# A later exponential, a sum at the end of the pass, and a shared ring of buffers, in the linear attention layer of a four-layer network

## The chip, the cores and the metric

The kernel runs on one core of a Trainium2 chip. The core has five engines with queues of their own: TensorE (PE, with its weight loads PEld), VectorE (DVE), ScalarE (ACT), GpSimd (POOL) and SyncE (SP, which here only issues transfers). They meet through semaphores. The metric is the device time of one execution in microseconds, the median over several runs.

## The reference

Sixteen images of 4096 tokens with 256 channels pass through four layers. Each is `x = x + layer(groupnorm(x))`:

- layer 0: a search for the nearest of 1024 code vectors for each token
- layer 1: row attention with a sigmoid
- layer 2: a gate from a softmax over all 4096 tokens
- layer 3: linear attention with a layer norm. The change lies in it:

```python
qkv = jnp.einsum('bxyc,cf->bxyf', x, w_qkv)
q, k, v = jnp.split(qkv, 3, axis=-1)
...
q = jax.nn.softmax(q, axis=-2) * SCALE
k = jax.nn.softmax(k, axis=-1)
context = jnp.einsum('bhdn,bhen->bhde', k, v)
out = jnp.einsum('bhde,bhdn->bhen', context, q)
...
out = jnp.einsum('bxyh,hc->bxyc', out, w_out) + b_out
mu = jnp.mean(out, axis=-1, keepdims=True)
var = jnp.mean(jnp.square(out - mu), axis=-1, keepdims=True)
out = (out - mu) * jax.lax.rsqrt(var + LN_EPS) * gamma + beta
```

The softmax of q runs over the 32 channels of a head; that of k over all 4096 tokens.

## The kernel before

All is float32. An image is cut into eight chunks of 512 tokens (`NCHUNK`), a chunk into four tiles of 128 (`CH`). The layers are Python generators (`stage1`, `layer1`, `rows2`, `stage2`, `gate2`, `stage3`), one set for each image. A heap at the end of the kernel steps through the generators of several images by due time: each `yield n` moves its generator on by n units, and a `stage3` has 160 of them (`task("layer3", ..., 160)`). So the search of one image is written between the exponentials of the one before and the attention of an older one. The order in which the code is thus written out is a priority: a planner then lays out each engine's queue, takes ahead what it holds ready, and on the chip each queue runs in the order laid out. Tiles with the same `tag` share `bufs` buffers, which are handed out in the order of the code.

`stage3` has two parts.

The **pass over k** (from L740): for each chunk `xt` is loaded (L742), PE forms k's scores `pk` (L747), DVE takes their maximum into the running `nkm` (L750, L753), ACT forms `al`, the factor by which older sums shrink (L754), and `kx`, the exponential of k, with its sum in `ks` (L756). POOL keeps the running sum: `ksum = ksum * al + ks` (L758, L759). PE forms queries and values, which ACT copies to `qv` (L769 to L774). In the second half of the chunk, after `yield 5`, `kx` is transposed and copied to `ek` (L780, L782). The queries of the chunk before, already normalized, are transposed (`queries`, L726), copied to `qT` (L728) and stored to DRAM by ACT's queue (L730). Then the maximum of this chunk's queries over each head is taken (DVE, L788), subtracted (POOL, L789), and the exponential taken in place (ACT, L790). PE forms `pc`, which joins the context `ctxa` (L794, L796). In the next chunk `normalize` sums the exponentials on DVE (L736), inverts, and multiplies on POOL (L738).

**Between** the parts the context is turned into the output weights `wctx` and their Gram matrix `gram` (L805 to L827), at raised priority; `rk = 1 / ksum` is used at L815.

The **output pass** (from L870): `fetch` loads a chunk of transposed queries back into `qo` (L834, on SP), `form` multiplies it by `gram` on PE (`pz`, L838) and with itself on DVE (`qz`, L840), `variance` sums the squares (L846) and raises to the power -1/2 on POOL (L849), `deviate` scales the queries (L856, L857). For each of two halves (`pr`) PE sums the transposed residual, the product with `wctx` and a row (`pxo`, L884 to L894), ACT copies to `y` (L895), and SP stores it (L905). `form` runs two chunks ahead, `fetch` three.

The tiles `kx`, `ek`, `qT` and `qz` share tag `v2` with four buffers; `qo` has three of its own, each of 2 KB per partition.

Of the kernel before, what the change touches and what calls it, by code (L numbers as in the profile page):

```python
# [9 lines left out]
F32 = mybir.dt.float32  # L10
BF16 = mybir.dt.bfloat16
U32 = mybir.dt.uint32
AF = mybir.ActivationFunctionType
ALU = mybir.AluOpType
AX = mybir.AxisListType

P = 128
# [4 lines left out]
CH = 4  # L22
NCHUNK = NT // CH
CW = CH * P
# [17 lines left out]
def kernel(  # L42
# [7 lines left out]
    nc = tc.nc  # L50
# [10 lines left out]
    s3p = ctx.enter_context(tc.tile_pool(name="s3p", bufs=2))  # L61
# [637 lines left out]
    def stage3(b):  # L699
        tag = f"s3_{b}"  # L700
# [21 lines left out]
        def queries(ch):  # L722
            qv = qvs.pop(ch)
            pq = bank(f"pq_{tag}_{ch}")
            for t in range(CH):
                nc.tensor.transpose(pq[:, t * P : (t + 1) * P], qv[:, t, 0, :], ident)  # L726
            qT = s3p.tile([P, CW], F32, tag="v2", name=f"qT_{tag}_{ch}", bufs=4)
            nc.scalar.activation(qT, pq, AF.Copy, scale=float(DH ** -0.5))  # L728
            qd_ = dram.tile([P, CW], F32, tag=f"qT_{ch}", name=f"qd_{tag}_{ch}")
            nc.scalar.dma_start(out=qd_, in_=qT)  # L730
            qTs.append(qd_)

        def normalize(ch):
            q4 = qvs[ch][:, :, 0, :].rearrange("p t (h d) -> p t h d", d=DH)
            qd = small.tile([P, CH, HEADS], F32, tag="qd", name=f"qd_{tag}_{ch}")
            nc.vector.tensor_reduce(qd, q4, AX.X, ALU.add)  # L736
            nc.vector.reciprocal(qd, qd)  # L737
            nc.gpsimd.tensor_tensor(q4, q4, qd.unsqueeze(3).to_broadcast([P, CH, HEADS, DH]), ALU.mult)  # L738

        for ch in range(NCHUNK):  # L740
            xt = xb.tile([P, NK, CW], F32, tag="xb", name=f"xk_{tag}_{ch}")
            nc.sync.dma_start(out=xt, in_=x3[ch])  # L742
            if ch > 0:
                normalize(ch - 1)
            pk = bank(f"pk_{tag}_{ch}")
            for k in range(NK):
                nc.tensor.matmul(pk, lhsT=wk_n[:, k, :], rhs=xt[:, k, :], start=(k == 0), stop=(k == NK - 1))  # L747

            now = nkm[:, ch : ch + 1]
            nc.vector.tensor_reduce(now, pk, AX.X, ALU.max, negate=True)  # L750
            if ch > 0:
                last = nkm[:, ch - 1 : ch]
                nc.vector.tensor_scalar(now, now, last, None, ALU.min)  # L753
                nc.scalar.activation(al[:, ch : ch + 1], last, AF.Exp, scale=-1.0, bias=now)  # L754
            kx = s3p.tile([P, CW], F32, tag="v2", name=f"kx_{tag}_{ch}", bufs=4)
            nc.scalar.activation(kx, pk, AF.Exp, bias=now, accum_out=ks[:, ch : ch + 1])  # L756
            if ch > 0:
                nc.gpsimd.tensor_tensor(ksum, ksum, al[:, ch : ch + 1], ALU.mult)  # L758
                nc.gpsimd.tensor_tensor(ksum, ksum, ks[:, ch : ch + 1], ALU.add)  # L759
            else:  # L760
                nc.gpsimd.tensor_copy(ksum, ks[:, 0:1])
            qv = s3p.tile([P, CH, 2, P], F32, tag="u4", name=f"qv_{tag}_{ch}")
            qvs[ch] = qv
            for pr in range(CH // 2):
                pqv = bank(f"pqv_{tag}_{ch}_{pr}").rearrange("p (j n) -> p j n", j=2)
                for j in range(2):
                    t = 2 * pr + j
                    for k in range(NK):
                        nc.tensor.matmul(  # L769
                            pqv[:, j, :], lhsT=xt[:, k, t * P : (t + 1) * P], rhs=wqv_n[:, k, :],  # L770
                            start=(j == 0 and k == 0), stop=False, skip_group_check=True,
                        )
                nc.tensor.matmul(pqv, lhsT=ones3, rhs=twice(qv_row), start=False, stop=True, skip_group_check=True)
                nc.scalar.copy(qv[:, 2 * pr : 2 * pr + 2, :, :].rearrange("p j s n -> p j (s n)"), pqv)  # L774
            if ch == 0:
                put_row(x_row, xm_, by_identity, f"x_{tag}", idle=8)
            yield 5
            pkt = bank(f"pkt_{tag}_{ch}")
            for t in range(CH):
                nc.tensor.transpose(pkt[:, t * P : (t + 1) * P], kx[:, t * P : (t + 1) * P], ident)  # L780
            ek = s3p.tile([P, CH, P], F32, tag="v2", name=f"ek_{tag}_{ch}", bufs=4)
            nc.scalar.copy(ek.rearrange("p t d -> p (t d)"), pkt)  # L782
            if ch > 0:
                queries(ch - 1)

            q4 = qv[:, :, 0, :].rearrange("p t (h d) -> p t h d", d=DH)
            qm = small.tile([P, CH, HEADS], F32, tag="qm", name=f"qm_{tag}_{ch}")
            nc.vector.tensor_reduce(qm, q4, AX.X, ALU.max)  # L788
            nc.gpsimd.tensor_tensor(q4, q4, qm.unsqueeze(3).to_broadcast([P, CH, HEADS, DH]), ALU.subtract)  # L789
            nc.scalar.activation(qv[:, :, 0, :], qv[:, :, 0, :], AF.Exp)  # L790

            pc = bank(f"pc_{tag}_{ch}")
            for t in range(CH):
                nc.tensor.matmul(pc[:, :P], lhsT=ek[:, t, :], rhs=qv[:, t, 1, :], start=(t == 0), stop=(t == CH - 1))  # L794
            if ch > 0:
                nc.vector.scalar_tensor_tensor(  # L796
                    ctxa, ctxa, al[:, ch : ch + 1], pc[:, :P], op0=ALU.mult, op1=ALU.add
                )
            else:
                nc.vector.tensor_copy(ctxa, pc[:, :P])  # L800
            yield 5
        normalize(NCHUNK - 1)
        rk = small.tile([P, 1], F32, tag="rk", name=f"rk_{tag}")
        nc.vector.reciprocal(rk, ksum)
        with tc.high_priority(offset=URGENT):  # L805
# [21 lines left out]
            nc.scalar.activation(gram, pw[:, :P], AF.Copy, scale=1.0 / C)  # L827
        yield 4
        queries(NCHUNK - 1)
        qs, prods, rss = {}, {}, {}  # L830

        def fetch(ch):
            qs[ch] = s3p.tile([P, CW], F32, tag="qo", name=f"qo_{tag}_{ch}", bufs=3)
            nc.sync.dma_start(out=qs[ch], in_=qTs[ch])  # L834

        def form(ch):
            pz = bank(f"pz_{tag}_{ch}")
            nc.tensor.matmul(pz, lhsT=gram, rhs=qs[ch], start=True, stop=True)  # L838
            prods[ch] = s3p.tile([P, CW], F32, tag="v2", name=f"qz_{tag}_{ch}", bufs=4)
            nc.vector.tensor_tensor(prods[ch], pz, qs[ch], ALU.mult)  # L840

        def variance(ch):
# [13 lines left out]
                nc.tensor.transpose(pd[:, t * P : (t + 1) * P], rs[:, t : t + 1].to_broadcast([P, P]), ident)  # L856
            nc.vector.tensor_tensor(qs[ch], pd, qs[ch], ALU.mult)  # L857

        fetch(0)
        fetch(1)  # L860
        form(0)
        yield 3
# [9 lines left out]
        for ch in range(NCHUNK):  # L872
            xt = xb.tile([P, NK, CW], F32, tag="xb", name=f"xo_{tag}_{ch}")
            nc.sync.dma_start(out=xt, in_=x3[ch])
            qT = qs[ch]
            y = s3p.tile([P, CH, C], F32, tag="u4", name=f"y_{tag}_{ch}")
            for pr in range(2):
                if pr == 1 and ch + 1 < NCHUNK:
                    deviate(ch + 1)
                px = bank(f"pxo_{tag}_{ch}_{pr}").rearrange("p (j c) -> p j c", c=C)  # L880
                for j in range(2):
                    t = 2 * pr + j
                    for k in range(NK):
                        nc.tensor.matmul(  # L884
                            px[:, j, k * P : (k + 1) * P], lhsT=xt[:, k, t * P : (t + 1) * P], rhs=ident,
                            is_transpose=True, start=(j == 0 and k == 0), stop=False, skip_group_check=True,
                        )
                for j in range(2):
                    t = 2 * pr + j
                    nc.tensor.matmul(  # L890
                        px[:, j, :], lhsT=qT[:, t * P : (t + 1) * P], rhs=wctx[:, 1, :], start=False, stop=False,
                        skip_group_check=True,
                    )
                nc.tensor.matmul(px, lhsT=ones3, rhs=twice(x_row), start=False, stop=True, skip_group_check=True)  # L894
                nc.scalar.copy(y[:, 2 * pr : 2 * pr + 2, :], px)  # L895
                if pr == 0:
                    if ch + 2 < NCHUNK:
                        form(ch + 2)
                else:
                    if ch + 2 < NCHUNK:  # L900
                        variance(ch + 2)
                    if ch + 3 < NCHUNK:
                        fetch(ch + 3)
                    if before is not None:
                        nc.sync.dma_start(out=dst[:, (ch - 1) * CH : ch * CH, :], in_=before)  # L905
                yield 3
            before = y
# [73 lines left out]
```

## Time and profile before

| what | us |
|---|---|
| median of three runs | 5770.42 (5766.87 to 5782.12) |
| the profiled execution | 5760.43 |
| its span in the profile | 5758.7 |
| L756 `kx`, ACT, 128 times, mean | 0.670 |
| L790 exponential of q, ACT, 128 times, mean | 0.627 |
| L789 subtraction, POOL, 128 times, mean | 1.572 |
| L758, L759 sum of k, POOL, 112 times each, mean | 0.906, 0.629 |
| L738 normalization, POOL, 128 times, mean | 1.593 |
| L838 `pz`, PE, all | 147.8 |
| L890 `pxo` with `wctx`, PE, all | 268.5 |
| L630 DVE and L627 ACT of the gate's softmax, 1024 times each, mean | 2.339, 2.089 |

The profile is of one execution. For each engine it gives the busy time, and the idle time before each group of instructions with what ended it. A table of waits sums these by pair ("who waited for whom": total, times, longest). The chain of waits follows the work that ended last back from the last instruction. The timeline lists single instructions, with the idle time before each in brackets. The granted TensorE clock was 0.958 of full speed on average.

### The profile page before, as it was taken

What the parts mean: (1) busy time and instruction counts of PE and PEld (TensorE: products, weight loads), DVE (VectorE), ACT (ScalarE), POOL (GpSimd) and SP (SyncE); (2) the same over time, 40 slices, a digit from 0 to 9 for tenths busy, and PEclk for the clock granted to TensorE, in tenths of its full rate; (3) what the DMA queues carried; (4) which work ended last, traced back from release to release, by engine and by line L of the source; (5) the groups of instructions that cost most, each with busy time, mean ns of one, the idle gap of its engine ahead of it and who ended that gap; (6) DMA issues with size and microseconds to landing.
All of it is one profiled execution on the core that took longest, in us unless ns stands there. A gap on an engine that the chain in (4) does not pass through costs nothing.

```text
span 5758.7 us, 80501 instructions
## 1 busy us (share of the span) xinstructions
PE 5245.1 (91%) x28975; PEld 3212.6 (56%) x28975; DVE 5067.1 (88%) x7154; ACT 4496.9 (78%) x6498; POOL 1930.8 (34%) x1314
## 2 busy tenths in 40 slices
PE   8978899989999999999999999999999999986887
PEld 3534455545656556565655656565565656564555
DVE  6489799998999999899999999999998999998872
ACT  4478597878888787887878888787888878887763
POOL 3123234223343343434334343332424333221231
PEclk9988999989999999999999999999999999998889
DMA  6443836655665756566575666656565664644543
GB/s 188 144 150 102 259 113 189 201 169 164 202 200 174 237 159 212 183 197 209 168 229 164 212 191 196 216 170 227 163 215 176 201 221 143 225 148 174 195 155 116
DMA packets 521382, 1059.53 MB, mean 184 GB/s; under 512 B 52504, under 2 KB 266392, under 8 KB 512792
## 3 DMA queue, kind: packets, MB, share of 16 engines
q1 hardware_dynamic: 406288, 885.11, 45.2%
q0 software_dynamic: 73728, 67.14, 8.1%
q10 hardware_dynamic: 40968, 102.13, 4.7%
q8 instruction: 230, 3.77, 0.3%
q14 instruction: 168, 1.38, 0.1%
HBM read 751.18 MB, written 303.04 MB: 183 GB/s over the span
## 4 chain that ended last, share of the span: by engine, by line
PE 40%; DVE 16%; ACT 9%; DMA 5%; issue 5%; POOL 3%; ACTq 0%; DVEq 0%; SPq 0%; POOLq 0%
PE pd_s L387 12%; DVE ex_s L630 7%; ACT ex_s L627 4%; PE ph_l L477 3%; PE pxo_s L890 3%; DMA qo_s<-qd_s 3%; PE po_l L515 2%; PE pqv_s L769 2%; PE pk_s L747 2%; PE pz_s L838 2%; POOL qv_s L789 2%; PE pxo_s L884 2%; DVE i_s L398 2%; DVE nn_s L393 1%; PE pvr_s L846 1%
## 5 line engine op out<-in xcount | busy, mean ns | idle before, releaser
L630 DVE CUSTOM_DVE_ANT_0 ex_s<-ex_s,x2b 128x2048 f32<-128x2048 f32 x1024 | 2387.1, 2339 | 69.5 <-ACT ex_s L627 69.1
L627 ACT ACTIVATE ex_s<-x0b,nmax_s,x_r 128x2048 f32<-128x2048 f32 x1024 | 2138.2, 2089 | 59.7 <-DVE num_s L630 48.0
L387 PE MATMUL pd_s<-e,xn_s 128*128 128x512 f32 x4096 | 1990.0, 620 | 62.7 <-DVE m L393 52.3
L399 POOL DMA_INDIRECT xc_s<-in_emb_rows,i_s x512 | 1097.6, 2144 | 1846.2 <-DVE i_s L398 1361.2
L387 PEld LDWEIGHTS pd_s<-e,xn_s 128*128 128x128 f32 x4096 | 747.2, 196 | 816.6 <-issue 680.7
L393 DVE CUSTOM_DVE_ANT_0 nn_s<-pd_s,nn_s 128x1024 f32<-128x1024 f32 x512 | 619.9, 1212 | 160.1 <-PE pd_s L387 86.9
L398 DVE FIND_INDEX8 i_s<-m,nn_s 128x8 uint32<-128x1024 f32 x512 | 623.2, 1218 | 0.0
L382 ACT ACTIVATE nn_s<-ne,nx_s 128x1024 f32<-128x1024 f32 x512 | 582.3, 1143 | 43.1 <-DVE nx_s L353 21.2
L477 PE MATMUL ph_l<-wh_l,xt_l 128*128 128x256 f32 x2048 | 520.6, 392 | 15.1 <-DVE m L393 10.0
L769 PE MATMUL pqv_s<-wqv_s,xk_s 128*128 128x256 f32 x2048 | 488.8, 380 | 0.0
L769 PEld LDWEIGHTS pqv_s<-wqv_s,xk_s 128*128 128x128 f32 x2048 | 388.8, 190 | 120.2 <-issue 60.1
L477 PEld LDWEIGHTS ph_l<-wh_l,xt_l 128*128 128x128 f32 x2048 | 382.2, 193 | 125.0 <-issue 59.3
L849 POOL TENSOR_TENSOR lrs_s<-lrs_s,mhalf 128x4 f32<-128x4 f32 x128 | 175.2, 1369 | 649.6 <-ACT lrs_s L848 640.3
L789 POOL TENSOR_TENSOR qv_s<-qv_s,qm_s 128x512 f32<-128x512 f32 x128 | 201.2, 1572 | 371.0 <-DVE qm_s L788 197.3
L738 POOL TENSOR_TENSOR qv_s<-qv_s,qd_s 128x512 f32<-128x512 f32 x128 | 203.9, 1593 | 280.9 <-DVE qd_s L737 160.8
L515 PEld LDWEIGHTS po_l<-at_l,h_l 64*128 64x128 f32 x4096 | 258.8, 192 | 59.4 <-issue 28.1
L515 PE MATMUL po_l<-at_l,h_l 64*128 64x64 f32 x4096 | 286.8, 281 | 5.4 <-DVE m L393 2.8
L895 ACT COPY y_s<-pxo_s 128x512 f32<-128x512 f32 x256 | 149.1, 583 | 164.8 <-PE pxo_s L894 146.2
L890 PE MATMUL pxo_s<-wctx_s,qo_s 128*128 128x256 f32 x1024 | 268.5, 385 | 0.0
L747 PE MATMUL pk_s<-xk_s,wk_s 128*128 128x512 f32 x512 | 256.0, 623 | 0.6 <-DMA xk_s<-x_g 0.4
L362 PE MATMUL pt_s<-ident,xc_s 128*128 128x128 f32 x1024 | 159.5, 287 | 99.2 <-DMA xc_s<-in_emb_rows,i_s 66.6
L332 ACT ACTIVATE xn_s<-xt_s,nb_n,s_n 128x512 f32<-128x512 f32 x256 | 200.5, 806 | 37.0 <-DMA xt_s<-in_xT 24.1
(201 smaller groups left out, 7471.3 us busy)
## 6 DMA issues: line engine op xcount, KB each, us to landing
xs_s<-in_xT SPq DMA_DIRECT2D x128, 512.0 KB
xt_s<-in_xT SPq DMA_DIRECT2D x128, 512.0 KB
xc_s<-in_x SPq DMA_DIRECT2D x128, 512.0 KB
x_s<-xt_s ACTq DMA_DIRECT2D x128, 512.0 KB
xt_l<-x_s SPq DMA_DIRECT2D x128, 512.0 KB
x_l<-xt_l SPq DMA_DIRECT2D x128, 512.0 KB
xr_r<-x_l SPq DMA_DIRECT2D x128, 512.0 KB
xg_g<-x_l SPq DMA_DIRECT2D x128, 512.0 KB
```

What stands on the lines that cost most here:

```text
L382: nc.scalar.activation(nn, ne2, AF.Identity, bias=nx2[ch][:, t : t + 1])
L387: nc.tensor.matmul(pd[:, cols], lhsT=xn[ch][:, k, t * P : (t + 1) * P], rhs=e2[:, k, cols], start=(k == 0), stop=(k == NK - 1),)
L393: nc.vector.tensor_tensor_reduce(out=nn, in0=pd, in1=nn, scale=1.0, scalar=-3.0e38, op0=ALU.add, op1=ALU.max, accum_out=m8[:, 0:1],)
L398: nc.vector.max_index(i8, m8, nn)
L399: nc.gpsimd.indirect_dma_start(out=xc[ch][:, t, :], out_offset=None, in_=emb_rows, in_offset=bass.IndirectOffsetOnAxis(ap=i8[:, 0:1], axis=0),
L477: nc.tensor.matmul(ph[:, t, :], lhsT=X[:, k, t * P : (t + 1) * P], rhs=wh_n[:, k, :], start=(t % 2 == 0 and k == 0), stop=False, skip_grou ...
L515: nc.tensor.matmul(po[:, r, k * CH + t, :], lhsT=h[rows, t, k * P : (k + 1) * P], rhs=at[rows, t, :], start=True, stop=True,)
L627: nc.scalar.activation(ex, x0b, AF.Exp, bias=nmax[:, T : T + 1], scale=x01[:, T, 1:2], accum_out=den[:, h, T : T + 1])
L630: nc.vector.tensor_tensor_reduce(out=ex, in0=ex, in1=x2b, scale=1.0, scalar=0.0, op0=ALU.mult, op1=ALU.add, accum_out=num[:, h, T : T + 1],)
L747: nc.tensor.matmul(pk, lhsT=wk_n[:, k, :], rhs=xt[:, k, :], start=(k == 0), stop=(k == NK - 1))
L769: nc.tensor.matmul(pqv[:, j, :], lhsT=xt[:, k, t * P : (t + 1) * P], rhs=wqv_n[:, k, :], start=(j == 0 and k == 0), stop=False, skip_group ...
L890: nc.tensor.matmul(px[:, j, :], lhsT=qT[:, t * P : (t + 1) * P], rhs=wctx[:, 1, :], start=False, stop=False, skip_group_check=True,)
```

## The change

- The exponential of the queries moves from its place behind the subtraction to the middle of the second half chunk: `yield 5` becomes `yield 2`, the exponential, `yield 3`.
- POOL's running sum of k goes. At the end of the pass one exponential gives each chunk's factor from its maximum to the last one, and DVE multiplies these with the chunks' sums `ks` and adds up.
- `qo` joins tag `v2`, which gets seven buffers in place of four; the tag `qo` with its three goes, so the memory is the same. `fetch(0)` is written right behind the pass, ahead of the work between the parts, and in the output pass `fetch(ch + 3)` is written in the first half of a chunk and not in the second.

```diff
-            qT = s3p.tile([P, CW], F32, tag="v2", name=f"qT_{tag}_{ch}", bufs=4)
+            qT = s3p.tile([P, CW], F32, tag="v2", name=f"qT_{tag}_{ch}", bufs=7)
...
             nc.scalar.activation(kx, pk, AF.Exp, bias=now, accum_out=ks[:, ch : ch + 1])
-            if ch > 0:
-                nc.gpsimd.tensor_tensor(ksum, ksum, al[:, ch : ch + 1], ALU.mult)
-                nc.gpsimd.tensor_tensor(ksum, ksum, ks[:, ch : ch + 1], ALU.add)
-            else:
-                nc.gpsimd.tensor_copy(ksum, ks[:, 0:1])
...
             nc.gpsimd.tensor_tensor(q4, q4, qm.unsqueeze(3).to_broadcast([P, CH, HEADS, DH]), ALU.subtract)
-            nc.scalar.activation(qv[:, :, 0, :], qv[:, :, 0, :], AF.Exp)
...
                 nc.vector.tensor_copy(ctxa, pc[:, :P])
-            yield 5
+            yield 2
+            nc.scalar.activation(qv[:, :, 0, :], qv[:, :, 0, :], AF.Exp)
+            yield 3
+        qs, prods, rss = {}, {}, {}
+
+        def fetch(ch):
+            qs[ch] = s3p.tile([P, CW], F32, tag="v2", name=f"qo_{tag}_{ch}", bufs=7)
+            nc.sync.dma_start(out=qs[ch], in_=qTs[ch])
+
         normalize(NCHUNK - 1)
+        fetch(0)
+
+        fac = small.tile([P, NCHUNK], F32, tag="al", name=f"fac_{tag}")
+        nc.scalar.activation(fac, nkm, AF.Exp, scale=-1.0, bias=nkm[:, NCHUNK - 1 :])
+        nc.vector.tensor_tensor(fac, fac, ks, ALU.mult)
+        nc.vector.tensor_reduce(ksum, fac, AX.X, ALU.add)
         rk = small.tile([P, 1], F32, tag="rk", name=f"rk_{tag}")
...
         queries(NCHUNK - 1)
-        qs, prods, rss = {}, {}, {}
-
-        def fetch(ch):
-            qs[ch] = s3p.tile([P, CW], F32, tag="qo", name=f"qo_{tag}_{ch}", bufs=3)
-            nc.sync.dma_start(out=qs[ch], in_=qTs[ch])
-
...
-        fetch(0)
         fetch(1)
         form(0)
...
                 if pr == 0:
                     if ch + 2 < NCHUNK:
                         form(ch + 2)
+                    if ch + 3 < NCHUNK:
+                        fetch(ch + 3)
                 else:
                     if ch + 2 < NCHUNK:
                         variance(ch + 2)
-                    if ch + 3 < NCHUNK:
-                        fetch(ch + 3)
```

`kx`, `ek` and `qz` get `bufs=7` in the same way.

## The prediction

> **What bounds the kernel now.** I read the page's busy shares first, then the stretches of one sample's length (busy time by engine), then the table of waits, the chain of waits, and the timeline where they pointed.
>
> ```profile
> PE 5245.1 (91%) x28975; PEld 3212.6 (56%) x28975; DVE 5067.1 (88%) x7154; ACT 4496.9 (78%) x6498; POOL 1930.8 (34%) x1314
> ...
> 4082.00:4422.00 340.00, 320.31 (x1820) 197.53 (x1820) 316.92 (x447) 281.69 (x409) 120.87 (x82) 0.99 0.62 196
> ...
> 5443.00:5758.00 315.00, 254.19 (x1223) 182.93 (x1223) 174.36 (x277) 171.03 (x295) 83.25 (x80) 0.89 0.41 137
> ```
>
> The stages of different samples overlap, and from 1360 to 4763 us the trace repeats every 340 us. In such a period (columns: length, then PE, PEld, DVE, ACT, POOL busy) PE works 320 us and DVE 317. Only some 20 us per sample can be won, and only where PE or DVE stands. The last stretch is looser: there one sample's output pass runs alone.
>
> ```profile
> ACT qv_s L790 <- POOL qv_s L789: 185.8, 79, 6.6
> POOL ksum_s L758 <- ACT al_s L754: 145.6, 55, 6.5
> PE pz_s L838 <- DMA qo_s<-qd_s: 39.7, 36, 3.1
> PE pq_s L726 <- POOL qv_s L738: 23.3, 12, 10.0
> SPq L834 <- DMA qd_s<-qT_s: 242.9, 44, 14.5
> ```
>
> These are totals, times, longest. The change touches all five: ACT waits before the queries' exponential, POOL before the running sum, PE for the reloaded queries, PE for the normalized queries, SP for a query store. Only the two PE rows are time on the bounding engine; the others must reach it.
>
> **The exponential and the sum (together).** One instance shows how a stall travels (start, length, engine, line):
>
> ```profile
> 2749.89 2.07 POOL L758 TENSOR_TENSOR ksum_s<-ksum_s,al_s 128x1 f32<-128x1 f32 x1
> ...
> 2752.17 3.11 POOL L789 TENSOR_TENSOR qv_s<-qv_s,qm_s 128x512 f32<-128x512 f32 x1
> ...
> 2755.32 0.63 ACT L790 ACTIVATE qv_s<-qv_s 128x512 f32<-128x512 f32 x1 [3.72 <-POOL qv_s L789]
> ...
> 2757.02 1.23 DVE L393 CUSTOM_DVE_ANT_0 nn_s<-pd_s,nn_s 128x1024 f32<-128x1024 f32 x1 [2.63 <-ACT nn_s L382]
> ...
> 2758.31 3.70 PE L387 MATMUL pd_s<-e,xn_s 128*128 128x512 f32 x8 [1.75 <-DVE m L393]
> ```
>
> The subtraction on POOL sits behind the 128x1 sum; ACT, whose queue is in order, stands 3.72 us; the search's ACT step behind it is late, so DVE stands 2.63 and PE 1.75: about half arrives. Over the ten repeating periods the PE waits that can have this cause are 27.8 us (pd behind DVE m), 14.6 (pt behind ACT qv) and 12.5 (px behind ACT sq). Counting half of the first and third, since other ACT work also precedes them, gives 35 us, 3.5 per sample, 52 over some 15 samples.
>
> How much of it goes? The exponential moves down by 2 of the 10 units of a chunk. The eight chunks of one pass take 188 us (2648 to 2836), so a unit is 2.35 us and the move at most 4.7 us. But the written order is only a preference: the trace's fetch of chunk 0, written after the whole pass, leaves at 2695, during the pass. A step that is ready on an idle ACT may keep its place. Removing the sum helps apart from that: L758 and L759 are 101.4 + 70.5 us of POOL, the copy 12.5, and in two of the five stalls of this period (2755, 2822) they stood right ahead of L789. Bounds: 0 (ACT stalls elsewhere) to 60 us; I take two thirds of 52, **-34 us**.
>
> The same POOL steps also meet DVE. The Trainium skill (SBUF — State Buffer, "SBUF: two separate sides") says a GpSimd step and a DVE step with two SBUF inputs exclude each other for a whole instruction, whichever starts second waiting. The row agrees from POOL's side: L758 is 0.18 us at its shortest and 2.07 here, L789 1.05 or 3.11. By the rule alone each of the 240 removed steps could have held DVE for its some 0.2 us: 48 us of DVE. The row shows DVE starting first (POOL pays) in the case above, and the large DVE step is busy 41% of the span: 20 us of DVE at most by that share, and DVE is not alone in bounding. I take **-8**, ends 0 and -48.
>
> What the sum costs instead, per sample: one exponential (as L754, 0.29 us on ACT), one small product and one small reduction (as L641 0.15 and L608 0.18 on DVE). They need the last chunk's maximum and sums. In the last pass those are ready at 5693.3, and the reciprocal is first used at 5699.38 (L815): 6 us of cover in which ACT and DVE have gaps. The new tile shares two buffers with `al`, free again a whole sample before they are due. Cost if the cover is gone: 16 x 0.62 = 10 us. I take **+3**. No new table switch: the page counts ACT_TABLE_LOAD once in 6498 ACT instructions, with Exp mixed in everywhere.
>
> **What the later exponential can cost.** Behind it hang the DVE sum L736, the POOL product L738 and PE's transposes pq. In the eight chunks from 2648 on, L738 ends ahead of pq by 2.0, 10.7, 0 (PE waits 0.92), 18, 6.2, 6.3, 4.2 and 0.8 us. A chunk that stalls today loses nothing until the slip exceeds its stall (3.3, 3.6, 0, 0, 3.7, 1.1, 0, 1.8). A full slip of 4.7 us costs PE 4.7 + 0.5 + 2.1 = 7.3 us per sample; a slip of 2 us costs 2. In the forecast the planner places pq, too, later, so it is put at 0 here and carried below as a rival.
>
> **The ring.** Before, `qo` has three buffers of its own, so fetch(ch+3) waits for the last matmul on qo(ch), and the product pz(ch+3) is due half a chunk later. After, seven shared buffers hold four qo and one or two qz in the output loop, so no slot is waited for, and the fetch leaves half a chunk sooner. On SP it passes the store of the previous y, which its 0.32 us of issue delays; nothing waits for that store in this while. The chain in the last pass:
>
> ```profile
> 5712.00 4.05 DMA qo_s<-qd_s
> 5716.19 1.10 PE pz_s L838 x2
> 5719.05 4.34 DMA qo_s<-qd_s
> 5723.53 1.10 PE pz_s L838 x2
> ```
>
> PE stands 1.64 us at 5716 and 1.93 at 5723 of a chunk of 7.3. The skill (DMA: Bandwidth & Descriptors, "Anatomy of one DMA") fits 2.0 us plus size over 436 GB/s, for GpSimd-issued transfers: 256 KB would be an estimated 2.6 us, landing at 5714.6, just as PE's earlier work ends, and an earlier fetch would bring nothing. The measured 4.05 decides (7.16 at 3248, under full load). PE's waits for it are 6.8 us in the last pass, 7.1 and 4.2 in the two passes before (5560 to 5612, 5395 to 5430), 14.9 in the ten periods. The first lies bare on the path; of the next two I take 60%, of the rest half: 6.8 + 6.8 + 7.4 = **-21 us**, ends -10 and -40. What is late next there is PE itself (5.1 to 5.8 us busy in 7), then the transfers: 1.28 MB per chunk in 5.3 us is 242 GB/s, just under the page's busiest slice, 259.
>
> The first three fetches lose ground. Buffers of one tag go out in the order of the code, so fetch(0) now follows the last kx, ek and qT6, fetch(1) follows qT7, fetch(2) the first product; before, they left early in the pass (2695, 2717, 2728) and waited on SP for their stores. In the last pass qT6 is written at 5696.16 and pz is due at 5701.95: 5.8 us for a 4 us transfer. fetch(1) (qT7 at 5702.06, pz at 5704.78) would be 1.4 us late if it really left behind qT7. In a period it has 7.1 us (qT7 at 2836.5, pz at 2843.6) against 7.2; fetch(2), behind the product at 2840.9 and due at 2857.8, has 17. Ends: 0 and 16 x 3 = 48 for a fetch(1) held up on SP; I take **+6**. SP no longer holds other loads behind those 243 us; no PE row of size hangs on them (pr 12.0, pfg 5.7), so 0, up to -15.
>
> **Sum.** -34 - 8 + 3 - 21 + 6 = -54. The profiled execution took 5760.4 (span 5758.7), so 5706; the median of the runs stands 10 us above it: **5716**.
>
> **Rivals.**
> - *The full gain* (0.10): every stall goes and the lock matters: -60 - 48 - 35, some -120 with overlap: 5650. For it: the chain gives L789 2% and qo 3%, 288 us. Against: PE has only 20 us per period to give, from a dozen causes.
> - *The exponential keeps its place* (0.10): the change does not do what it says; the sum and the ring remain, with a third of the stalls: -12 - 8 - 21 + 9 = -32: 5738.
> - *Off the path* (0.17): in the periods another queue comes due at once; only the last passes gain: 5760 - 14, so 5756 on the median.
> - *The wait moves to pq* (0.21, slower): exp slips by its full 4.7 us, and PE waits for the normalized queries: 16 x 7.3 = +117, net +63: 5833. It decides from where it eats the gain of 54, 3.4 us per sample, a slip of about 3 us. For it: two of eight chunks have under 1 us to spare. Against: the slip fills time in which ACT stands today.
>
> **How the numbers follow.** The forecast has 0.42, own range 5690 to 5745. The full gain and most of the kept-place case add to faster, off the path and the rest of that case to no change (0.3% is about what a measurement of this kernel tells from none): 0.60, 0.19, 0.21. The range 5650 to 5810 takes in the full gain as priced, the middle, and the milder half of the slower case.
>
> **What would show it.** Right: ACT's wait before the exponential under 70 us, PE's for qo under 10, the last pass's chunk near 5.4 us, periods near 337. Wrong: pq's wait on L738 over 60 us, or pz's wait for qo grown at the first chunks; periods of 340 would mean off the path. Above all, a queue order that shifts elsewhere, in the search or the gate, can outweigh all of this.

## The result, and the profile after

| | before | after |
|---|---|---|
| median, 12 runs each on one chip | 5768.65 us (5754.86 to 5782.12) | 5758.13 us (5744.93 to 5784.61) |
| ratio, 95% interval | | 0.9991 [0.9978, 1.0004] |
| the same again, on another occasion | 5766.81 us, 46 runs | 5752.20 us, 21 runs: 0.9977 [0.9964, 0.9989] |
| profiled execution | 5760.43 us | 5752.8 us |
| its span; mean granted clock of TensorE | 5758.7 us; 0.958 | 5750.7 us; 0.951 |

The forecast was 54 us less. What came is 10 to 15 us by the medians: no change that this measurement can tell, or just at its edge.

First the page's busy row after the change:

```profile
PE 5265.1 (92%) x28975; PEld 3236.0 (56%) x28975; DVE 5084.4 (88%) x7186; ACT 4499.1 (78%) x6514; POOL 1720.1 (30%) x1074
```

and the stretch of one sample and the last stretch from the table of windows (length, then PE, PEld, DVE, ACT, POOL busy, then clock, DMA share, GB/s):

```profile
4082.00:4422.00 340.00, 321.83 (x1843) 198.50 (x1845) 320.74 (x453) 283.97 (x414) 108.29 (x68) 0.99 0.62 195
5443.00:5750.00 307.00, 255.71 (x1218) 184.34 (x1216) 172.10 (x275) 167.12 (x293) 67.84 (x50) 0.88 0.41 140
```

POOL has its 211 us of work less. PE has the same 28975 products as before, but they take **20 us longer** (5265.1 against 5245.1). PE's idle time, span less busy, fell from 513.6 to 485.6: 28 us were won there, and 20 of them went back into longer products. These are two single executions, and their clocks (0.958, 0.951) lie a little further apart than the means over the runs do. In the stretch of one sample PE and DVE are some 322 and 321 us busy of 340, as full as before; the periods were not shortened.

Three waits from before that are not shown yet, then the waits after the change (total, times, longest):

```profile
POOL qv_s L789 <- DVE qm_s L788: 197.3, 71, 6.1
...
PE pd_s L387 <- DVE m L393: 52.3, 43, 6.1
...
PE ph_l L477 <- DVE m L393: 10.0, 9, 1.5
```

```profile
POOL qv_s L784 <- DVE qm_s L783: 515.9, 74, 30.9
...
ACT qv_s L796 <- POOL qv_s L784: 162.4, 70, 6.0
...
PE pd_s L387 <- DVE m L393: 31.7, 19, 8.1
...
PE pq_s L726 <- POOL qv_s L738: 18.7, 9, 10.0
...
PE pz_s L840 <- DMA qo_s<-qd_s: 18.6, 14, 3.4
PE ph_l L477 <- DVE m L393: 18.6, 9, 2.9
```

ACT's wait for the subtraction, which the change aims at, is 162.4 instead of 185.8, hardly less. POOL, freed of the sum, now stands 515.9 us before the subtraction for DVE's maximum, up from 197.3: idle time of an engine that isn't the bound. PE's wait for the reloaded queries fell by 21 us (39.7 to 18.6), that for the search's maximum by 21 (52.3 to 31.7), and the attention's `ph` (L477) waits 9 us more than its 10.0.

In the chain of waits, the last pass now runs like this, PE's `pz` of successive chunks with no transfer between them:

```profile
5714.89 0.86 PE pz_s L840 x2
...
5720.06 0.86 PE pz_s L840 x2
```

5.17 us for a chunk, where it was 7.2 to 7.3. So the ring does at the end what was said. The gain of this execution by stretches, from the starts of each sample's last y copy: samples 0 and 1 gain 12.7 us, the last four 11.6, and the ten repeating periods between **lose 16.6** (338.1 to 339.8 us each).

### The profile page after: what moved, and what is told of

It is laid out like the page before. It is cut to its first block, busy times and chain, and to the rows that moved or that the text cites. A ratio compares the mean times of both kernels' runs of the same rounds, so it can differ in the third digit from the quotient of the medians.

```text
span 5750.7 us, 80113 instructions
## 1 busy us (share of the span) xinstructions
PE 5265.1 (92%) x28975; PEld 3236.0 (56%) x28975; DVE 5084.4 (88%) x7186; ACT 4499.1 (78%) x6514; POOL 1720.1 (30%) x1074
## 4 chain that ended last, share of the span: by engine, by line
PE 41%; DVE 16%; ACT 10%; issue 5%; DMA 4%; POOL 3%; SPq 0%; ACTq 0%; DVEq 0%; POOLq 0%
PE pd_s L387 12%; DVE ex_s L630 7%; ACT ex_s L627 5%; PE ph_l L477 4%; PE pxo_s L891 3%; PE pqv_s L764 3%; PE pk_s L747 2%; PE po_l L515 2%; PE pxo_s L885 2%; PE pz_s L840 2%; DMA qo_s<-qd_s 2%; DVE nn_s L393 2%; DVE i_s L398 2%; PE pvr_s L848 1%; POOL qv_s L784 1%
## 5 line engine op out<-in xcount | busy, mean ns | idle before, releaser
L387 PE MATMUL pd_s<-e,xn_s 128*128 128x512 f32 x4096 | 1986.4, 620 | 42.1 <-DVE m L393 31.7
L477 PE MATMUL ph_l<-wh_l,xt_l 128*128 128x256 f32 x2048 | 531.7, 397 | 31.3 <-DVE m L393 18.6
L477 PEld LDWEIGHTS ph_l<-wh_l,xt_l 128*128 128x128 f32 x2048 | 386.6, 196 | 147.9 <-issue 72.9
L784 POOL TENSOR_TENSOR qv_s<-qv_s,qm_s 128x512 f32<-128x512 f32 x128 | 197.9, 1546 | 716.8 <-DVE qm_s L783 515.9
L851 POOL TENSOR_TENSOR lrs_s<-lrs_s,mhalf 128x4 f32<-128x4 f32 x128 | 161.6, 1262 | 676.8 <-ACT lrs_s L850 662.3
```

Source lines behind the costliest of these rows:

```text
L387: nc.tensor.matmul(pd[:, cols], lhsT=xn[ch][:, k, t * P : (t + 1) * P], rhs=e2[:, k, cols], start=(k == 0), stop=(k == NK - 1),)
L477: nc.tensor.matmul(ph[:, t, :], lhsT=X[:, k, t * P : (t + 1) * P], rhs=wh_n[:, k, :], start=(t % 2 == 0 and k == 0), stop=False, skip_grou ...
```

## The experiments

All times are medians; the ratio is to the kernel before, measured beside it. "Clock" is the mean of the granted clock over the runs. A last column sets the runs of one kernel against their clocks (a straight line through them) and reads the time at 0.954. Such a line falls 41 to 64 us per 0.01 of clock, 48 in the middle (27 in more_filler), with correlations of 0.64 to 0.99.

| run | median us | ratio [95%] | clock | at clock 0.954 |
|---|---|---|---|---|
| before | 5767 to 5773 | 1 | 0.955 to 0.957 | 5777 to 5780 |
| ring_only | 5763.91 | 0.9993 [0.9978, 1.0008] | 0.9543 | 5768 |
| sum_only | 5740.77 | 0.9951 [0.9936, 0.9967] | 0.9582 | 5759 |
| exp_only | 5757.77 | 0.9979 [0.9960, 0.9998] | 0.9544 | 5761 |
| no_subtraction | 5676.76 | 0.9834 [0.9807, 0.9861] | 0.9548 | 5680 |
| sum_and_ring | 5734.43 | 0.9941 [0.9925, 0.9958] | 0.9560 | 5746 |
| sum_and_exp | 5748.11 | 0.9965 [0.9953, 0.9976] | 0.9556 | 5756 |
| exp_and_ring | 5744.19 | 0.9970 [0.9955, 0.9984] | 0.9531 | 5743 |
| after_again | 5752.20 | 0.9977 [0.9964, 0.9989] | 0.9522 | 5746 |
| no_filler | 5772.77 | 1.0004 [0.9989, 1.0019] | 0.9446 | 5722 |
| no_shift_sum_ring | 5609.04 | 0.9733 [0.9710, 0.9756] | 0.9604 | 5638 |
| more_filler | 5749.08 | 0.9969 [0.9958, 0.9981] | 0.9576 | 5759 |
| normalize_late_only | 5716.65 | 0.9903 [0.9883, 0.9922] | 0.9572 | 5734 |
| exponential_at_half_end | 5720.74 | 0.9900 [0.9875, 0.9926] | 0.9573 | 5733 |
| later_alone | 5710.18 | 0.9892 [0.9867, 0.9918] | 0.9557 | 5721 |
| later_exponential | 5683.04 | 0.9857 [0.9835, 0.9879] | 0.9580 | 5700 |

The values at an equal clock are a reading of mine, good to some 3 to 8 us (the scatter about the lines was 1 to 10). They take it that the clock sets the time of a run; that a run with longer waits gets a lower clock would give such a line too, and the two were not told apart; where a kernel's clocks lie far from 0.954, as in no_filler and no_shift_sum_ring, they are read off outside the measured range. The ratios are what was measured.

### Each part alone

The three parts of the diff, each applied to the kernel before (the ring with its earlier fetches), and that kernel without the subtraction:

```diff
# ring_only
-            kx = s3p.tile([P, CW], F32, tag="v2", ..., bufs=4)
+            kx = s3p.tile([P, CW], F32, tag="v2", ..., bufs=7)
...
-            qs[ch] = s3p.tile([P, CW], F32, tag="qo", ..., bufs=3)
+            qs[ch] = s3p.tile([P, CW], F32, tag="v2", ..., bufs=7)
# sum_only
-                nc.gpsimd.tensor_tensor(ksum, ksum, al[:, ch : ch + 1], ALU.mult)
-                nc.gpsimd.tensor_tensor(ksum, ksum, ks[:, ch : ch + 1], ALU.add)
...
+        nc.scalar.activation(fac, nkm, AF.Exp, scale=-1.0, bias=nkm[:, NCHUNK - 1 :])
+        nc.vector.tensor_tensor(fac, fac, ks, ALU.mult)
+        nc.vector.tensor_reduce(ksum, fac, AX.X, ALU.add)
# exp_only
-            nc.scalar.activation(qv[:, :, 0, :], qv[:, :, 0, :], AF.Exp)
...
-            yield 5
+            yield 2
+            nc.scalar.activation(qv[:, :, 0, :], qv[:, :, 0, :], AF.Exp)
+            yield 3
# no_subtraction
-            nc.gpsimd.tensor_tensor(q4, q4, qm..., ALU.subtract)
```

> Only the ring of seven and the earlier fetches. Theory A (the change's gain in the last passes and in the first ones, where few samples overlap, comes from the fetches; in the repeating periods the order of the queues decides): 0.3 to 0.4% faster than before (some 5740 to 5755), the last pass's chunk 5.2 us in place of 7.2, PE's wait for qo under 20 us. Rival B (all three parts gain a little and the granted clock takes it back): about 0.1% faster, with a mean clock below that of before.

> Only the sum of k at the end of the pass. Theory A: within 0.2% of before; POOL's busy time falls by some 185 us and ACT's wait before the exponential by less than 30 us, since the subtraction then waits for DVE's maximum. Rival B: 0.2 to 0.4% faster, ACT's wait before the exponential under 140 us.

> Only the exponential written two units later. In the queue laid out, 83 of its 128 instances keep their place. Theory A: ACT's wait for the subtraction stays over 140 us and the time within 0.3% of before, either way. Rival C (the wait moves to the normalized queries): 0.5% or more slower, PE's wait at pq for L738 over 40 us against 23.

> The kernel before without the subtraction of the queries' maximum on POOL (left out; the maximum itself is still formed), so that ACT has nothing to wait for before the exponential: what ACT's 186 us of standing and POOL's 201 us are worth at most. If the prediction's mechanism holds (about a third of ACT's standing reaches PE): 0.6 to 1.2% faster, PE's idle time down by 35 us or more. If the standing is off the path: within 0.3% of before.

Measured: the ring 0.07% (its interval includes 1), the sum 0.49%, the exponential 0.21%, which would be 0.77% together, and the three together bring 0.09 to 0.23%. So the sum of the parts is not the whole, and **one part alone, the sum, beats the change**. ACT's waits before the exponential in sum_only, exp_only and no_subtraction, against 185.8 us before:

```profile
ACT qv_s L785 <- POOL qv_s L784: 170.0, 79, 5.6
```

```profile
ACT qv_s L801 <- POOL qv_s L789: 182.0, 85, 5.9
```

```profile
ACT qv_s L789 <- DVE qm_s L788: 44.7, 30, 3.1
```

The sum gained more than either expectation gave it, with a stall only 16 us shorter. Without the subtraction ACT still waits 44.7 us, now for DVE's maximum, and 1.66% or some 96 us goes. That is near twice the 52 us of reach that the prediction gave the stall. It is a value for the stall at most: POOL's 201 us of subtractions go with it, and the queues are laid out anew (some 780 of ACT's other 6370 instructions stand in another order). What these two brought was not measured apart.

### The parts in pairs

Edits: the hunks above, two at a time; after_again is the changed kernel.

> The sum at the end and the ring, the exponential in its old place. Theory 'the clock takes it back': at an equal granted clock the gains add up, 13 us for the ring and 22 for the sum, so about 35 us below before; what is measured differs from that by 48 us per 0.01 of granted clock, so with the clock of the sum alone (0.958) 5735, with that of the changed kernel (0.9505) 5772. Rival 'the parts get in each other's way in the queues': stalls of PE come back at an unchanged clock, so the time is above 5760 though the clock stays at 0.956 or more.

> The sum at the end and the later exponential, without the ring. Theory 'the clock takes it back': 22 + 19 = 41 us below before at an equal granted clock, so 5730 at a clock like before's, 5758 where it falls by 0.006 as in the changed kernel. If the ring is what lowers the clock (its first fetches leave later, and two waits of over 3 us for them are followed by 13.7 us at half clock each in the changed kernel), this kernel keeps a clock of 0.955 or more and is 0.4 to 0.7% faster than before. Rival 'parts in each other's way': over 5755 at a clock of 0.956 or more.

> The later exponential and the ring, with POOL's running sum kept. Theory 'the clock takes it back': 13 + 19 = 32 us below before at an equal clock; as both parts alone had a clock of 0.954, some 0.002 below before, about 5745 to 5760. Rival 'parts in each other's way': as slow as before or slower at a clock of 0.956 or more.

> The changed kernel once more, beside the pairs on one chip. Theory 'the clock takes it back': its granted clock is again lower than that of before by 0.004 or more, and the time again within 0.3% of before. If the clock's fall was only chance in the first measurement, the clock is the same as before's here and the time some 36 us (0.6%) below it.

At an equal clock the ring adds to the others as expected: sum_and_ring 33 us below before (35 expected), exp_and_ring 36 (32 expected). The sum and the exponential do not add: 24 in place of 41, hardly more than the sum alone (21). Why is not shown; ACT's stall itself fell by 31 us in sum_and_exp (to 155.2), more than by the sum (16) and the exponential (4) alone. And at the clock that each kernel really had, the later exponential costs: sum_and_ring takes 5734, the changed kernel, which is that plus the exponential, 5752, while at clock 0.954 both read 5746. The clock's fall in the changed kernel (0.9522 against 0.9566) came again and wasn't chance. In the rows of waits one difference can be seen; sum_and_ring has

```profile
ACT qv_s L785 <- POOL qv_s L784: 161.9, 78, 5.9
...
PE ph_l L477 <- DVE m L393: 12.1, 9, 1.8
```

ACT's stall is 161.9 us there with the exponential in its old place, 162.4 in the changed kernel: in this pair the move takes nothing from it. In the three others it takes 4 us (exp_only), 15 (sum_and_exp against sum_only) and 22 (exp_and_ring against ring_only), so at most an eighth. But `ph`, longest wait 1.8 us, waits up to 2.9 with the move.

### What a longer wait of the matrix engine costs

The records of the granted clock hold two values only, 1.0 and 0.5. Two instances of the same eight products of `ph` from the timelines (start, length, engine, line; idle before in brackets), first in the kernel before:

```profile
2096.27 1.97 PE L477 MATMUL ph_l<-wh_l,xt_l 128*128 128x256 f32 x8 [1.26 <-issue]
```

and then in the changed one:

```profile
2095.29 3.65 PE L477 MATMUL ph_l<-wh_l,xt_l 128*128 128x256 f32 x8 [2.13 <-issue]
```

The wait is 0.87 us longer, and the same eight products take 1.68 us longer: in the records a stretch at half clock begins at 2095.4. In this pair 0.87 us more of waiting cost 2.55. But a wait of 1.26 us can be followed by one too, as in another period of the kernel before:

```profile
2438.53 3.25 PE L477 MATMUL ph_l<-wh_l,xt_l 128*128 128x256 f32 x8 [1.26 <-issue]
```

So one such wait is no rule; the count is. `ph` waits 1.26 to 1.32 us in each of the ten periods of the kernel before, and a half-clock stretch follows in three of them; it waits 2.13 to 2.53 us in the changed kernel, and a stretch follows in seven.

The records show what goes with half clock. All stretches of a trace between 1360 and 4763 us begin on a grid of 3.41 us and last 3.41 us or a multiple of it. In these windows of the grid I added up PE's idle time, whatever it waited for. Of the full-clock windows with over 1.8 us of it, about half the window, all were followed by half clock, 7 in the kernel before and 17 in the changed one (over all seventeen traces 188 of 205); of those with under 1 us, 7 of 873 and 8 of 879. So what a wait costs also hangs on where it falls in the grid. Idle time is not all: in the kernel before five stretches follow windows in which PE never stood, filled for the most part with its small products (`po`, `psc`, `pvr`).

A longer case, timeline and windows of the changed kernel:

```profile
2574.08 2.05 PE L840 MATMUL pz_s<-qo_s,gram_s 128*128 128x512 f32 x2 [3.36 <-DMA qo_s<-qd_s]
```

```profile
2560.00:2573.00 13.00, 10.72 (x54) 7.45 (x52) 12.10 (x16) 9.44 (x14) 2.59 (x2) 1.00 0.85 247
2573.30:2586.90 13.60, 12.82 (x80) 9.29 (x81) 8.08 (x10) 6.31 (x9) 3.36 (x1) 0.50 0.46 161
2587.00:2600.00 13.00, 13.00 (x66) 8.24 (x65) 12.86 (x20) 7.21 (x11) 2.91 (x2) 1.00 0.68 215
```

A reloaded chunk of queries (chunk 6 of its output pass) lands 3.36 us late, a half-clock stretch begins during that wait, and PE works 13.6 us at clock 0.50, DVE and ACT thinning out beside it (8.08 and 6.31 us busy of 13.6). A second such place stands at 3928. Added up over 1360 to 4763 us, the half-clock stretches are 113 us before and 171 after (160 in after_again). By an estimate from these numbers, 58 us more at half clock is 29 us of PE's work; the periods lost 16.6, so without it they would have gained some 12. In the Trainium skill (TensorE: Matmul & The Clock Gate, "Part 1: The HAM clock gate") the same two states and a window of some 3.4 us stand, free-running; "HAM oscillation" there names idle gaps over that length as what turns the clock down. The grid of the trace agrees with the window; the limit of the trace is lower, some 1.8 us of idle time in one window.

To see whether the clock is a cause and not only a sign, I took the kernel's own filler products away, and added some:

```diff
# no_filler (on the changed kernel)
-        for _ in range(n):
+        for _ in range(0):
             nc.tensor.matmul(t[:, :512], lhsT=ones3, ...)
# more_filler (on the changed kernel)
-        busy(pg, 3 if kind == "n0" else 0)
+        busy(pg, 3 if kind == "n0" else 2)
...
             pt = bank(f"pct_{tag}")
+            busy(pt, 2)
```

(more_filler has the same two for `prt`, `pw`, `pwt` and `pgr`.)

> The changed kernel without its 224 filler products of TensorE (`busy`, 0.24 us each, 53 us of PE in all), which are written where PE waits for a short chain and whose results are overwritten. Theory 'the granted clock is a cause of time': the clock falls below that of the changed kernel (0.952) by 0.004 or more, and the time rises by 10 us or more, to 5762 and above, although PE has 53 us less to do. Rival 'the clock only mirrors how busy PE is': the time stays or falls by up to 53 us, whatever the clock.

> The changed kernel with 288 filler products more (two each ahead of the other group norms' means, of the gate's row transposes, and of each of four steps between the pass over k and the output pass), some 68 us of PE at 0.24 us each, mostly where PE waits. Theory 'the granted clock is a cause of time': the clock rises by 0.003 or more and the time falls or stays within 10 us of 5752, since each 0.01 of clock is worth 48 us and most of the fillers lie in waits. Rival 'the clock only mirrors how busy PE is': the time rises by a good part of 68 us, to 5785 or more.

PE's busy rows of no_filler, after_again and more_filler, one after the other:

```profile
PE 5274.1 (91%) x28751; PEld 3239.3 (56%) x28751; DVE 5061.8 (88%) x7186; ACT 4500.3 (78%) x6514; POOL 1745.9 (30%) x1074
```

```profile
PE 5259.3 (92%) x28975; PEld 3230.7 (56%) x28975; DVE 5081.8 (89%) x7186; ACT 4499.0 (78%) x6514; POOL 1723.2 (30%) x1074
```

```profile
PE 5314.3 (92%) x29263; PEld 3255.4 (57%) x29263; DVE 5087.7 (88%) x7186; ACT 4503.1 (78%) x6514; POOL 1709.4 (30%) x1074
```

With 224 products fewer PE is busy 15 us *longer* than in after_again, the clock is 0.9446, and the time is 20.6 us above the changed kernel's (the kernel before stood at 5767 beside both). The fillers took 59 us of PE there (60 in the first profile), so the products that stayed take some 74 us longer, more than the kernel lost; half-clock stretches are 661 us in place of 541. Less work and more time: the clock is a cause. The edit also lets the queues be laid out anew (ACT has another instruction at 1217 of its 6514 places); what that adds or takes was not measured apart. More fillers lift the clock to 0.9576 and leave the time as it was (5749 against 5752); what the clock gives, the 55 us of PE time take. So the lost clock isn't simply bought back with fillers at these places.

### An exponential that really moves

In the order in which ACT's instructions are laid out, about 90 of 128 exponentials of the changed kernel stand just as far behind their `ek` (L777) as before. One chunk of the changed kernel's timeline:

```profile
2093.12 0.68 DVE L783 TENSOR_REDUCE qm_s<-qv_s 128x16 f32<-128x512 f32 x1
...
2093.94 1.05 POOL L784 TENSOR_TENSOR qv_s<-qv_s,qm_s 128x512 f32<-128x512 f32 x1 [6.09 <-DVE qm_s L783]
...
2095.02 0.63 ACT L796 ACTIVATE qv_s<-qv_s 128x512 f32<-128x512 f32 x1 [2.00 <-POOL qv_s L784]
```

Maximum, subtraction, exponential, each at the end of the one before: ACT stands 2.00 us with the exponential at the head of its queue, as if nothing had been moved. So the exponential of a chunk was put behind the next chunk's `kx`:

```diff
# later_exponential (on the changed kernel)
-            if ch > 0:
-                normalize(ch - 1)
             pk = bank(f"pk_{tag}_{ch}")
...
             nc.scalar.activation(kx, pk, AF.Exp, bias=now, accum_out=ks[:, ch : ch + 1])
+            if ch > 0:
+                qp = qvs[ch - 1][:, :, 0, :]
+                nc.scalar.activation(qp, qp, AF.Exp)
+                normalize(ch - 1)
...
-            yield 2
-            nc.scalar.activation(qv[:, :, 0, :], qv[:, :, 0, :], AF.Exp)
-            yield 3
+            yield 5
+        nc.scalar.activation(qv[:, :, 0, :], qv[:, :, 0, :], AF.Exp)
```

> The changed kernel with the queries' exponential of a chunk written only behind the next chunk's exponential of k, and the normalization behind it, so that the queue can't easily keep the old place. Theory 'the move hardly moves it': in the changed kernel 90 of 128 exponentials keep their place, so here ACT's wait for POOL's subtraction, 162 us there, falls under 80; the time says what the true move is worth, and with the stall chain gone it should be 5735 or less. Rival 'the wait moves to the transposes of the normalized queries': PE's wait for POOL's L738, 18.7 us there, goes over 60 us and the time over 5780. Rival 'off the path': ACT's wait falls, and the time stays within 0.2% of the changed kernel.

5683.04: **1.43% below before**. Its waits, with the last chunk's exponential at a line of its own (L798):

```profile
ACT qv_s L757 <- POOL qv_s L786: 76.8, 36, 5.5
...
PE pq_s L726 <- POOL qv_s L738: 35.6, 23, 10.0
...
ACT qv_s L798 <- POOL qv_s L786: 8.2, 4, 4.5
```

ACT's stall is halved, 85 us in place of 162. PE's wait for the normalized queries does grow, from 18.7 to 35.6: the wait that the slower rival spoke of, at a seventh of its price (17 us of 117). The clock is 0.9580. The periods are 333.8 us. This moved the normalization too, so three runs more took the two apart:

```diff
# normalize_late_only: sum_and_ring, and
-            if ch > 0:
-                normalize(ch - 1)
             pk = bank(f"pk_{tag}_{ch}")
...
+            if ch > 0:
+                normalize(ch - 1)
             qv = s3p.tile([P, CH, 2, P], F32, tag="u4", ...)
# exponential_at_half_end: sum_and_ring, and
-            nc.scalar.activation(qv[:, :, 0, :], qv[:, :, 0, :], AF.Exp)
...
             yield 5
+            nc.scalar.activation(qv[:, :, 0, :], qv[:, :, 0, :], AF.Exp)
# later_alone: the edit of later_exponential on the kernel before
```

> The sum at the end and the ring, the exponential in its old place behind the subtraction, and only the normalization written behind the next chunk's exponential of k. 119 of 128 exponentials keep their place in ACT's queue. Theory 'the exponential's place is what counts': as the sum and the ring without this, 5734, within 0.3% (5717 to 5752), and ACT's wait for the subtraction stays at 140 us or more. Rival 'it was the normalization's place': most of the 1.2% that later_exponential lies below the changed kernel is there, 5683 to 5700.

> The changed kernel with the exponential written at the end of the half chunk (5 units later in place of 2), the normalization in its old place. By the queue written out, 90 of 128 exponentials then stand at another place than before, in the changed kernel 38. Theory 'the exponential's place is what counts': ACT's wait for the subtraction falls under 80 us and the time to about that of later_exponential, 5683 (5670 to 5700). Rival 'it was the normalization's place': as the changed kernel, 5740 to 5760. Rival 'the wait moves to the transposes of the normalized queries': PE's wait for L738 over 60 us, and over 5760.

> The kernel before with the exponential of a chunk written behind the next chunk's exponential of k and the normalization behind it; the running sum on POOL and the four and three buffers stay. Theory 'the place is what counts, the sum works on the same stall': 0.9 to 1.3% below before (5692 to 5715), ACT's wait for the subtraction under 100 us. Rival 'the sum on POOL must go first': the subtraction stays late behind the sum, ACT's wait over 130 us, and less than 0.5% gained.

ACT's and PE's rows of normalize_late_only, and those of exponential_at_half_end:

```profile
ACT qv_s L785 <- POOL qv_s L784: 159.5, 77, 6.7
PE pq_s L726 <- POOL qv_s L738: 34.1, 21, 10.0
```

```profile
ACT qv_s L796 <- POOL qv_s L784: 107.6, 44, 5.0
...
PE pq_s L726 <- POOL qv_s L738: 29.1, 18, 10.0
```

Later_alone has 97.7 us of this wait. Neither theory was right alone; the gains add up. From sum_and_ring (0.59% below before), the later normalization takes it to 0.97%, the later exponential to 1.00%, and later_exponential, which moves both (the exponential further still), to 1.43%; each is good to some 0.2%. The first leaves ACT's stall as it was (159.5), so its gain is another. DVE's sum over the heads and POOL's product no longer stand ahead of k's maximum in the order written; that this is what helps was not tried. Later_alone takes 1.08% without the ring and without touching POOL's sum, so the move of both needs neither.

### Neither maximum nor subtraction

```diff
# no_shift_sum_ring: sum_and_ring, and
-            nc.vector.tensor_reduce(qm, q4, AX.X, ALU.max)
-            nc.gpsimd.tensor_tensor(q4, q4, qm..., ALU.subtract)
```

> The kernel before with the sum at the end and the ring, the exponential in its old place, and with the maximum over a head's channels neither formed nor subtracted: the queries' softmax is computed from the exponentials of the raw scores. If the stall of ACT before that exponential is what the change is about, this takes it away whole: no_subtraction was 1.7% faster than before, the sum and the ring 0.6%; they work on partly the same stall, so 5655 to 5690 (1.3 to 2.0% below before). If they are independent, 2.3%: 5634. DVE's maximum, 128 times 0.68 us, goes as well, which is worth up to 87 us more where DVE bounds.

5609.04, **2.67% below before** and the shortest of all. The exponential there waits for nothing on POOL, and the wait of PE for the normalized queries is

```profile
PE pq_s L726 <- POOL qv_s L738: 4.1, 6, 0.7
```

The periods are 328.3 us. That is 25 us below the lowest of the estimates made without DVE's share, so something more came through: some of DVE's 87 us, or the clock (0.9604, the highest of all); this was not taken apart. It needs scores whose exponentials stay in float32's range, as those of these inputs do.

## Why the prediction was wrong

It foretold 5716, with 0.60 on a gain clear of the noise. That its range holds the 5758 measured is owed to its width. It gave the exponential with the sum 39 us (-34 - 8 + 3), and sum_and_exp measured 20 [14, 27]; it gave the ring 15 (-21 + 6), and ring_only measured 4 [-5, 13]. By its steps:

- **The exponential and the sum, -34: the step that failed.** It took two thirds of 52 us, as if the move ended most of ACT's stall. The stall lost 23 of 186 us. The prediction named the reason itself, that the written order is only a preference, but gave the kept place 0.10: about 90 of 128 exponentials kept theirs. Where the exponential really moves, 162 us of stall fall to 85 and the time by 69 (later_exponential, with the normalization moved). The sum alone was worth 28 us.
- **The reach of the stall, 52 us**, was too small, as far as is shown. Half of two PE waits that fitted the mechanism was counted, and the third whole; no_subtraction gave 96 at most. There PE's idle time falls by 78 us, also in waits that the prediction did not count: `pkt` for ACT's `kx` from 19.5 to 6.6 us, `psc` for ACT's `qv` from 11.9 to 0.
- **The lock between POOL and DVE, -8:** not seen. DVE is busy 17 us more, not less, and the POOL product takes 1.60 us as before.
- **The sum's new steps, +3:** right in kind. They take 4.6, 2.1 and 2.2 us in all 16 passes together, and PE's waits before `pct`, `pw`, `pwt` and `pgr` grew from 14.3 to 18.8 us.
- **The ring, -21, and the first fetches, +6:** sized well, as waits. By place in the output pass, PE's waits for chunks 3 to 5 fell from 19.9 us to nothing and those for chunk 1 rose from 0 to 5.0, in all 21 us less; the last pass went to 5.17 us a chunk (5.4 foretold). In time the ring alone is worth 4 us [-5, +13]. What stayed is chunk 6, with 12.3 us of it, and among them two waits of 3.4 and 3.2 us, each with 13.7 us at half clock.
- **What had no step: the granted clock.** The prediction priced a PE wait at its length. The clock fell by 0.0044 to 0.006, which at 48 us per 0.01 is an estimated 21 to 28 us, about half of the forecast. Read at an equal clock the change gains some 33 us of the 54; the rest of the miss lies in the steps above.
- **The rivals.** "The exponential keeps its place" had the mechanism, at 5738 where 5752 to 5758 came. "Off the path" had the number, 5756, and the periods (340), but for another reason, which is luck: the stall stayed where it was, and later_exponential shows that 1.4% was to be had from that path. "The wait moves to pq" was wrong by sign: in the changed kernel that wait is shorter (18.7 us, 23.3 before), and in later_exponential it grows by 17 us and the kernel still gains.

Open is why a move of 2 units lowers the clock and one of 5 doesn't (0.952 against 0.957). The changed kernel has more windows with over 1.8 us of idle time (17 against 7, though 11 in after_again), and `ph` is part of it: the stretches behind its waits grow from 10 us to 27, 17 of the 58. But `ph` waits up to 2.6 us in later_exponential too, where half clock takes 130 us of the periods, and the profiled run of sum_and_ring, with `ph` at 1.8, has 174 us and 16 such windows.

## What to carry to other kernels

When a written order is only a preference, look in the queue laid out for what really moved before pricing a move: here a move of 2 units was worth 0.2% alone and nothing on top of the others, and one past the next chunk's work, with the normalization, over 1%. Price a wait of the matrix engine at more than its length where it leaves the engine idle for over half of a window of 3.41 us, because a stretch at half clock follows. And measure the parts of a change apart: one of the three beat the whole.

## What was not expected of the hardware

- Half clock came by windows of 3.41 us, and followed nearly every window with over 1.8 us of PE idle time (188 of 205 in all traces). Eight products then took 3.65 us in place of 1.97.
- In the kernel before it also came five times behind windows in which PE never stood, filled for the most part with small products.
- Runs of one and the same kernel differ in their mean clock (0.951 to 0.961 in 43 runs of before), and their times go with it, some 48 us per 0.01 (correlation 0.80 in these runs, 0.66 in 46 others); which of the two follows the other was not tried.
- 224 products fewer on PE made PE busy 15 us longer and the kernel 20.6 us slower.
